# A graph layer's block pipeline: PSUM split by writer, sums a block later, layers two blocks later

## The chip, the core and the metric

The kernel runs on one core of a Trainium2 chip. The metric is the device time of one execution in microseconds, the median of three runs. A core has engines that run their own instruction streams and wait for each other by semaphores: TensorE (PE, matrix products, results into PSUM), VectorE (DVE), ScalarE (ACT), GpSimd (POOL) and SyncE (SP). Here POOL does almost nothing but issue gathers (indirect DMAs), SP and ACT issue DMAs, DVE does all the elementwise work.

## The reference

N = 50,000 nodes with D = 128 features, 1,650,000 edges sorted by destination, each of one of two types. Every edge sends its source's row through the weight matrix of its type; the messages are summed at the destination, a self term is added, then ReLU, a residual, and a layer norm.

```python
def _L0_gnn_ref(X, edge_index, edge_types, W_data, b_data, W_control, b_control, W_self, b_self):
    src = edge_index[0]
    dst = edge_index[1]
    Xs = X[src]
    m_data = Xs @ W_data.T + b_data
    m_ctrl = Xs @ W_control.T + b_control
    msg = jnp.where((edge_types == 0)[:, None], m_data, m_ctrl)
    agg = jax.ops.segment_sum(msg, dst, num_segments=X.shape[0])
    out = agg + (X @ W_self.T + b_self)
    return jax.nn.relu(out)

x = _layernorm(x + _L0_gnn_ref(x, edge_index, edge_type_2, ...), axis=-1)
```

## The kernel before

**Tiling.** The sorted edges are cut into 514 blocks (`NBLK`). A block is two steps (`Q`) of 12 chunks of 128 edges (`R`, `P`), so 24 chunks; each chunk's source rows are fetched by one gather of POOL (L555) into a buffer `y`. Besides these 3,072 edges a step takes 46 edges by "fill": edges of other places in the stream that are put into chunk rows which would have held a self loop (`F`, with `LATE` more for lateness), and 24 by single rows: DMAs of 512 bytes each, 12 issued by SP and 12 by ACT per step, so 24 each per block (L515 to L531), into `yx`. A block covers at most 112 destination nodes (`B`), a step at most 60 (`W`).

**Sums by product.** For each chunk, TensorE multiplies the gathered rows with a one-hot matrix `oh` (which of 60 destinations, which of two types) into a PSUM tile `acc`, one per step, accumulating over 12 chunks (`products`, L574), then the 24 single rows (L580), then the edge counts per destination and type for the biases (L583). A pass is six chunks (`PASS`), so a block has four passes, q = 0 to 3, and each pass has its own `y` from a ring of ten (`SLOTS`). `acc` comes from a ring of four, that is two blocks' worth. The gathers of a pass wait until the products that read the same buffer ten passes earlier are done; the first product of a pass waits for its six gathers.

**The rest of a block.** DVE adds each step's `acc` into the block's `sums` (`add`, L588; three `sums` tiles in turn). `begin_sums` (L599) starts a block's `sums` from the overlapping part of the block before and from `pl`, the correction for the self loops that the fill left out. `layer` (L613, L615) multiplies the finished sums by the two weight matrices into `po`, where `own_part` (L604, L605) has put the self term and the transposed row of `x`. `moments` (L620 to L628) takes ReLU, residual and mean and variance; `root` is a square root on ACT per two blocks, `store` (L647, L650) normalizes, `store_rows` (L655) writes 112 rows out from SP.

**Preparation.** Every ten blocks (`GB`) a group's edge lists are loaded and `columns` works out columns and ranks, for which TensorE makes `rank` (L298, L300) in a PSUM bank of its own from `h_loop` (L293, L294); DVE reads it at L323. Per block: `spread` (TensorE, L365) writes a list `vf` into the PSUM tile `small`; `fill` (DVE, L374 to L395) matches it, five blocks ahead (`RAHEAD`), giving the gathers' indices `idx` and `by`, the columns left out; `left_out_columns` (TensorE, L402) sums `by` into a column of `small`; `left_out_matrix` (DVE, L409, L410) reads that into `at` and makes `z`; `left_out_numbers` (TensorE, L418, L421) makes `pl` from `z`; `left_out_rows` (DVE, L427) multiplies `pl` by `xT`, a slice of transposed `x` that `positions` copies (L480) from a window `xw`. `onehot` and `counts` (DVE, L486, L494) make `oh` and `cnt` two blocks ahead (`AHEAD`); `onehot` reads a row of numbers, `num_ps`, that lies in the same PSUM tile `small` as `vf`, a copy `cb` (L374) and the sums of L402.

**Order.** Each engine runs its instructions in the order in which the code emits them; the framework puts a semaphore wait between an instruction and the last one on another engine that touched the same tile or, in PSUM, the same bank. One turn of the main loop, b, emits:

- before the passes: `spread` of the next fill, `add` of step 1 of block b-1, `begin_sums(b)`, `offsets`, `onehot(b+2)`, `counts(b+2)`
- pass 0, then `left_out_columns` and the `fill`, then 24 single rows on SP and ACT
- pass 1, then `layer(b-1)`, `left_out_numbers(b+1)`, `add` of step 0 of b, `moments(b-1)`, `left_out_matrix`, `positions(b+1)`, `left_out_rows(b+1)`, `store`
- pass 2 (with `columns` of the next group once in ten blocks), pass 3, `root`, `store_rows`

The adds read the `acc` of step 1 right after the last pass, at the start of the next turn, and that of step 0 after pass 1 of the same turn.

## Time and profile before

| | |
|---|---|
| median of three runs | 17,999.62 us (17,992.94 to 18,001.46) |
| the profiled execution's own time | 17,956.11 us |
| its span in the profile | 17,954.0 us |
| instructions in the trace | 165,064 |
| mean granted TensorE clock | 0.544 |
| gathers of POOL in the trace | 12,312 |
| moved by DMA | 913.88 MB, 51 GB/s on the mean |
| the chain of work that ended last | DVE 48%, unknown queue 27%, issue 15%, PE 10% |

The page's first part gives each engine's busy time and its share of the span. In a group's row, `out<-in` names the tiles, `x` counts instructions, then come the total busy time, the mean of one in ns, and the idle time of the engine just before these instructions with what ended it: "remote" is a message from another engine that the profile does not name, "issue" is time in which the engine waited for nothing that the profile shows. PEld is TensorE's loading of weights, which runs beside the products. A timeline row has the start, the duration, the engine and line, and in brackets the idle time ahead of it.

### The profile page before, as it was taken

What the parts mean: (1) busy time and instruction counts of PE and PEld (TensorE: products, weight loads), DVE (VectorE), ACT (ScalarE), POOL (GpSimd) and SP (SyncE); (2) the same over time, 40 slices, a digit from 0 to 9 for tenths busy, and PEclk for the clock granted to TensorE, in tenths of its full rate; (3) what the DMA queues carried; (4) which work ended last, traced back from release to release, by engine and by line L of the source; (5) the groups of instructions that cost most, each with busy time, mean ns of one, the idle gap of its engine ahead of it and who ended that gap; (6) DMA issues with size and microseconds to landing.
All of it is one profiled execution on the core that took longest, in us unless ns stands there. A gap on an engine that the chain in (4) does not pass through costs nothing.

```text
span 17954.0 us, 165064 instructions
## 1 busy us (share of the span) xinstructions
PE 8584.6 (48%) x37659; PEld 7319.4 (41%) x37660; DVE 12266.2 (68%) x14661; ACT 79.5 (0%) x264; POOL 11657.6 (65%) x12341
## 2 busy tenths in 40 slices
PE   4444444444444444444444444444444444544444
PEld 3444434444444444344444443444444443444434
DVE  7676666666666766666666676666666666766765
ACT  0000000000000000000000000000000000000000
POOL 6666666666666666666666666666666666666666
PEclk6555555555555555555555555555555555555555
DMA  2111212112122121111212211212221121121111
GB/s 54 51 50 51 52 50 51 51 51 51 50 52 51 50 52 50 51 51 51 51 50 52 51 50 51 51 51 51 51 51 50 51 52 50 51 52 50 51 50 50
DMA packets 529268, 913.88 MB, mean 51 GB/s; under 512 B 232762, under 2 KB 315875, under 8 KB 528274
## 3 DMA queue, kind: packets, MB, share of 16 engines
q0 software_dynamic: 394592, 808.89, 17.8%
q1 hardware_dynamic: 108668, 87.80, 1.7%
q10 hardware_dynamic: 25014, 6.54, 0.2%
q8 instruction: 306, 5.01, 0.1%
q14 instruction: 688, 5.64, 0.1%
HBM read 872.82 MB, written 29.47 MB: 50 GB/s over the span
## 4 chain that ended last, share of the span: by engine, by line
DVE 48%; another core or an unknown queue 27%; issue 15%; PE 10%; DVEq 0%; SPq 0%; DMA 0%; ACT 0%; ACTq 0%
DVE cnt L494 13%; DVE oh L486 7%; PE acc L574 7%; DVE m L376 4%; DVE v_new L383 4%; DVE new L379 4%; DVE old L392 4%; DVE sums L588 1%; DVE z L410 1%; DVE h L621 1%; DVE st L623 1%; PE acc L580 1%; PE po L615 1%; DVE xT L480 1%
## 5 line engine op out<-in xcount | busy, mean ns | idle before, releaser
L555 POOL DMA_INDIRECT y<-in_x,idx x12312 | 11638.2, 945 | 6265.2 <-issue 3408.4
L574 PEld LDWEIGHTS acc<-oh,y 128*128 128x128 f32 x24662 | 5348.8, 314 | 8255.9 <-issue 7977.9
L574 PE MATMUL acc<-oh,y 128*128 128x120 f32 x24662 | 5960.7, 412 | 3728.7 <-issue 3722.8
L588 DVE TENSOR_TENSOR sums<-acc,sums 128x180 f32 x1028 | 349.9, 340 | 4032.1 <-remote 3704.4
L494 DVE TENSOR_REDUCE cnt<-oh 128x240 bf16<-128x3120 f32 x514 | 3008.8, 5854 | 17.9
L402 PE MATMUL small<-ones_b,by 128*112 128x1 bf16 x512 | 83.4, 163 | 4177.0 <-issue 4045.0
L486 DVE TENSOR_TENSOR oh<-col,small 128x3120 f32<-128x3120 f32 x514 | 1740.6, 3386 | 43.8 <-remote 39.5
L395 DVE TENSOR_REDUCE by<-old 128x112 bf16<-128x1456 f32 x512 | 1426.7, 2787 | 17.5
L376 DVE TENSOR_TENSOR m<-rk,small 128x1456 f32<-128x1456 f32 x512 | 855.7, 1671 | 20.7 <-remote 2.4
L379 DVE TENSOR_TENSOR new<-m,small 128x1456 f32<-128x1456 f32 x512 | 855.2, 1670 | 17.5
L383 DVE TENSOR_REDUCE v_new<-new 128x26 f32<-128x1456 f32 x512 | 854.9, 1670 | 17.5
L392 DVE TENSOR_TENSOR old<-m,small 128x1456 f32<-128x1456 f32 x512 | 852.0, 1664 | 0.0
L580 PE MATMUL acc<-oh,yx 24*128 24x120 f32 x2048 | 758.1, 465 | 82.1 <-issue 82.1
L620 DVE COPY h<-po 112x128 f32<-112x128 f32 x514 | 145.3, 283 | 738.9 <-remote 622.6
L580 PEld LDWEIGHTS acc<-oh,yx 24*128 24x128 f32 x2048 | 487.3, 291 | 330.2 <-issue 319.1
L615 PE MATMUL po<-wmsgT,sums 128*112 128x128 f32 x2056 | 613.4, 453 | 3.7 <-issue 3.7
L365 PE MATMUL small<-v_f,row_of 10*128 10x112 bf16 x1536 | 223.2, 270 | 590.3 <-DVE at L409 197.6
L615 PEld LDWEIGHTS po<-wmsgT,sums 128*112 128x112 f32 x2056 | 448.8, 297 | 130.6 <-issue 129.9
L613 PE MATMUL po<-bias,sums 3*112 3x128 f32 x1028 | 391.4, 482 | 0.5 <-DVE sums L588 0.4
L365 PEld LDWEIGHTS <-row_of 10*128 10x128 bf16 x1536 | 122.8, 111 | 634.5 <-issue 592.7
L300 PEld LDWEIGHTS <-ones_b 128*128 128x128 bf16 x624 | 78.7, 149 | 671.3 <-issue 659.8
L298 PE MATMUL rank<-h_loop,below 128*128 128x260 bf16 x52 | 19.5, 375 | 672.7 <-DVE h_loop L294 357.8
(145 smaller groups left out, 5094.1 us busy)
## 6 DMA issues: line engine op xcount, KB each, us to landing
y<-in_x,idx POOLq DMA_INDIRECT x12312
yx<-in_x ACTq DMA_DIRECT2D x12288, 0.5 KB
yx<-in_x SPq DMA_DIRECT2D x12288, 0.5 KB
xw<-in_x_t SPq DMA_DIRECT2D x65, 448.0 KB
out<-o SPq DMA_DIRECT2D x514, 56.0 KB
sdt<-in_edges_t SPq DMA_DIRECT2D x52, 390.0 KB
one_g<-in_src_x SPq DMA_DIRECT2D x52, 1.9 KB
sdt_f<-in_edges_f SPq DMA_DIRECT2D x52, 13.1 KB
```

Source lines behind the costliest of these rows:

```text
L376: nc.vector.tensor_tensor(m, rk_g[g][:, i, :, None].to_broadcast([P, C1, FX]), rank_no_ps[:, None, :].to_broadcast([P, C1, FX]), op=ALU.is ...
L379: nc.vector.tensor_tensor(new.rearrange("p (q r) f -> p q r f", r=R1), m.rearrange("p (q r) f -> p q r f", r=R1), vf.rearrange("p (q f) -> ...
L383: nc.vector.tensor_reduce(v, new, AX.X, ALU.add)
L392: nc.vector.tensor_tensor(old, m, cb[:, :, None].to_broadcast([P, C1, FX]), op=ALU.mult)
L395: nc.vector.tensor_reduce(by, old.rearrange("p (q r) f -> p q f r", r=R1), AX.X, ALU.add)
L486: nc.vector.tensor_tensor(oh, col_g[g][:, i, :, None].to_broadcast([P, C1, 2 * W]), num_ps[:, None, :].to_broadcast([P, C1, 2 * W]), op=AL ...
L494: nc.vector.tensor_reduce(cnt, ohs[b].rearrange("p (q r) w -> p q w r", r=R1), AX.X, ALU.add)
L555: copy = nc.gpsimd.indirect_dma_start(out=y[:r, k % PASS, :].bitcast(U8), out_offset=None, in_=x_rows, in_offset=bass.IndirectOffsetOnAxis ...
L574: nc.tensor.matmul(acc[:, :2, :].rearrange("p t w -> p (t w)"), y[:r, k % PASS, :], ohs[b][:r, column(k), :], start=k == of_step[0], stop= ...
L580: nc.tensor.matmul(acc[:, :2, :].rearrange("p t w -> p (t w)"), ys[b][:, q, :], ohs[b][:S, q * R1 + R, :], start=False, stop=True)
L588: nc.vector.tensor_tensor(part, accs.pop((b, q)), part, op=ALU.add)
L615: nc.tensor.matmul(po, a[:, t, :B], c["wmsgT"][:, t * D:(t + 1) * D], start=False, stop=t == 1)
```

## The change

Four things are changed at once.

1. The PSUM tile `small` and `rank`'s bank become two tiles by the engine that writes them: `fixed` (DVE writes it: `num_ps`, `rank_no_ps` and the copies `cb`, now `olds`) and `made` (TensorE writes it: `vf`, `rank` and the sums of left-out columns). `vf` was two lists in turn and is now one.
2. `columns` is split: `loops` makes `h_loop` and `ranks` queues the rank products, one turn ahead of `columns`, which reads `rank`.
3. The order of a turn is new. Spread and fill stand back to back before pass 0. Both adds of a block, its `begin_sums`, `left_out_rows` and `positions` are emitted one turn later, after pass 2; the layer and the moments two blocks later than the products; `left_out_columns` after pass 2, behind `left_out_matrix` of the fill before.
4. `oh` and `cnt` have four buffers instead of three, `by` four instead of two, `xw` two instead of three. The first and last blocks are written out to match.

```diff
-    ohp = ctx.enter_context(tc.tile_pool(name="ohp", bufs=AHEAD + 1))
+    ohp = ctx.enter_context(tc.tile_pool(name="ohp", bufs=AHEAD + 2))
...
-    ps_r = ctx.enter_context(tc.tile_pool(name="ps_r", bufs=1, space=bass.MemoryType.PSUM))
...
-    small = keep_ps.tile([P, 2 * W + FX + 2 * FILL + 2], F32, name="small")
-    num_ps, rank_no_ps = small[:, :2 * W], small[:, 2 * W:2 * W + FX]
-    lists = [small[:, 2 * W + FX + i * FILL:][:, :FILL] for i in range(2)]
-    sums_at = [small[:Q * FX, 2 * W + FX + 2 * FILL + i:][:, :1] for i in range(2)]
+    fixed = keep_ps.tile([P, 2 * W + FX + 2 * C1], F32, name="fixed")
+    num_ps, rank_no_ps = fixed[:, :2 * W], fixed[:, 2 * W:2 * W + FX]
+    olds = [fixed[:, 2 * W + FX + i * C1:][:, :C1] for i in range(2)]
+    made_ps = keep_ps.tile([P, Q * FX + GS * (R + 1) + 2], F32, name="made")
+    vf_ps, rank = made_ps[:, :Q * FX], made_ps[:, Q * FX:Q * FX + GS * (R + 1)].rearrange("p (s r) -> p s r", r=R + 1)
+    sums_at = [made_ps[:Q * FX, Q * FX + GS * (R + 1) + i:][:, :1] for i in range(2)]
...
+    def loops(g):
...
+        nc.vector.tensor_tensor(h[:, :, :, :R], a["s"].rearrange(steps, r=R1)[:, :, :, :R],
+                                a["d"].rearrange(steps, r=R1)[:, :, :, :R], op=ALU.is_equal)
...
+    def ranks(g):
...
+        nc.tensor.matmul(rank, below, hs_, start=True, stop=False)
...
-        by = fil.tile([P, Q, FX], BF16, name="by")
+        by = fil.tile([P, Q, FX], BF16, name="by", bufs=4)
...
-        xw = stp.tile([P, WIDE], F32, name="xw")
+        xw = stp.tile([P, WIDE], F32, name="xw", bufs=2)
...
-        for f in fresh:
-            spread(f)
-        if b > 0:
-            add(b - 1, steps_of(b - 1)[-1])
-        begin_sums(b)
...
         offsets(b + AHEAD + 1)
         if b + AHEAD < NBLK:
             onehot(b + AHEAD)
             counts(b + AHEAD)
-        last = steps_of(b)[-1:]
+        if i == GB // 2 - 2 and g + 1 < GROUPS:
+            loops(g + 1)
+        for f in fresh:
+            spread(f)
+            fill(f)
         for q, (step, ks) in enumerate(passes_of(b)):
             if ks:
                 products(b, step, ks)
-            if q == 0:
+            if q == 1 and b > 0:
+                if b > 1:
+                    layer(b - 2)
+                left_out_numbers(b - 1)
+            if q == 2:
+                for f in late_pcs:
+                    left_out_matrix(f)
                 for f in due:
                     left_out_columns(f)
-                for f in fresh:
-                    fill(f)
-            if q == 1 and b > 0:
-                layer(b - 1)
-            if q == 1:
-                left_out_numbers(b + 1)
-            if ks and step not in last and ks[-1] == chunks_of(b, step)[-1]:
-                add(b, step)
-            if q == 1 and b > 0:
-                moments(b - 1)
-            if q == 1:
-                for f in due:
-                    left_out_matrix(f)
-            if q == 1 and b + 1 < NBLK:
-                positions(b + 1)
-                left_out_rows(b + 1)
-            if q == 2 and i == GB // 2 - 1 and g + 1 < GROUPS:
-                columns(g + 1)
-            if q == 1 and b > 1 and pair(b - 2):
-                store(pair(b - 2))
-                ready.extend(pair(b - 2))
+                late_pcs = due
+                if i == GB // 2 - 2 and g + 1 < GROUPS:
+                    ranks(g + 1)
+            if q == 2 and b > 0:
+                positions(b - 1)
+                left_out_rows(b - 1)
+                begin_sums(b - 1)
+                for step in steps_of(b - 1):
+                    add(b - 1, step)
+                if b > 1:
+                    moments(b - 2)
...
+                if b > 1 and pair(b - 2):
+                    root(pair(b - 2))
+                if i == GB // 2 - 1 and g + 1 < GROUPS:
+                    columns(g + 1)
             if q < LOADS and not plain(b + AHEAD):
                 single_rows(b + AHEAD, q)
-            if q == 3 and b > 0 and pair(b - 1):
-                root(pair(b - 1))
             if q == 3 and ready:
                 store_rows(ready.pop(0))
```

The rows below are the engines' orders in the middle of the program; in brackets stand the semaphores that a row waits for, named by the engine that raises them (`landed` is raised by gathers, `fetched` by single rows). Lines of the changed kernel are up to 8 higher: L402 of before is L409, L574 is L581, L588 is L595, L421 is L428, L486 is L493.

TensorE around passes 0 to 1 of one block, before:

```order
L365 MATMUL small<-v_f,row_of 128x112 [waits DVE_49]
...
L574 MATMUL acc<-oh,y 128x120 [waits landed8,PE_sequencer_49]
L574 MATMUL acc<-oh,y 128x120 x5
L402 LDWEIGHTS by
L402 MATMUL small<-ones_b,by 112x1 [waits DVE_49]
L574 MATMUL acc<-oh,y 128x120 [waits landed9,PE_sequencer_49]
L574 MATMUL acc<-oh,y 128x120 x5
```

TensorE from the layer after pass 1 to the first product of the next block, in the changed kernel:

```order
L622 MATMUL po<-wmsgT,sums_189 112x128 x2
...
L428 MATMUL pl<-z,to_row 128x128
...
L581 MATMUL acc<-oh,y 128x120 [waits landed0,PE_sequencer_49]
L581 MATMUL acc<-oh,y 128x120 x5
L409 LDWEIGHTS by
L409 MATMUL made<-ones_b,by 112x1 [waits DVE_49]
L581 MATMUL acc<-oh,y 128x120 [waits landed1,PE_sequencer_49]
...
L373 MATMUL made<-v_f,row_of 128x112
...
L581 MATMUL acc<-oh,y 128x120 [waits landed2,PE_sequencer_49,DVE_49]
```

The sum of left-out columns has moved from after pass 0 to after pass 2, with another wait for DVE ahead of it, and the first product of a block now waits for DVE as well.

VectorE over one block, before:

```order
L427 TENSOR_TENSOR pl<-pl,xT 128x2x112 [waits DVE_49,PE_49]
...
L588 TENSOR_TENSOR sums_191<-acc,sums_191 128x3x60 [waits PE_49]
...
L599 TENSOR_TENSOR sums_189<-pl,sums_191 128x3x112 [waits DVE_49]
...
L486 TENSOR_TENSOR oh<-col,small 128x3120 [waits PE_49]
...
L374 COPY small<-cb 128x26 [waits PE_49]
...
L395 TENSOR_REDUCE by<-old 128x112 [waits DVE_49]
...
L588 TENSOR_TENSOR sums_189<-acc,sums_189 128x3x60 [waits PE_49]
L620 COPY h<-po 112x128 [waits PE_49]
```

VectorE over one block, in the changed kernel:

```order
L402 TENSOR_REDUCE by<-old 128x112 [waits DVE_49]
L416 COPY at<-made 112x1
...
L434 TENSOR_TENSOR pl<-pl,xT 128x2x112 [waits DVE_49,PE_49]
...
L606 TENSOR_TENSOR sums_189<-pl,sums_188 128x3x112 [waits DVE_49]
...
L595 TENSOR_TENSOR sums_189<-acc,sums_189 128x3x60 [waits DVE_49]
...
L627 COPY h<-po 112x128
...
L493 TENSOR_TENSOR oh<-col,fixed 128x3120
...
L386 TENSOR_TENSOR new<-m,made 128x1456 [waits DVE_49,PE_49]
```

The adds, the one-hot matrix and the copy into `h` no longer wait for TensorE themselves; the product on `pl`, ahead of them, and `new` in the fill do.

More of the change, by code (lines that the diff above doesn't have):

```diff
@@ L174, in straight @@
     loads = {}
+    hs_g = {}
     col_g, rk_g, stay_g, cb_g, vp_g, late_g = {}, {}, {}, {}, {}, {}
@@ L288, in first_of_f @@
                    begin_p.rearrange("b (q g) -> b q g", q=Q)[:, :, g:g + 1].to_broadcast([GB, Q, FX]))
[L292 to L301 removed]
+        hs_ = hs_g.pop(g)
         col, rel, nz = columns_of(a["d"], a["t"], first_of, "")
@@ L688, in find_bad @@
         nc.vector.tensor_copy(c["bad"], total)
+    loops(0)
+    ranks(0)
     columns(0)
```

95 lines of the change are left out of this document (51 added, 44 removed).

## The prediction

> **What bounds the kernel now.** I read the page's first part, then the groups, the waits, the timeline of a block in the middle, and its windows. The profiled execution took 17,956 us (span 17,954.0); the median of the three timed runs is 43 us (0.24%) above it. The sums below are made against the execution, and the 43 us come on at the end.
>
> Rows of the page, then of the view by lines and of the waits (us in total, times, longest):
>
> ```profile
> PE 8584.6 (48%) x37659; PEld 7319.4 (41%) x37660; DVE 12266.2 (68%) x14661; ACT 79.5 (0%) x264; POOL 11657.6 (65%) x12341
> ...
> L555 POOL DMA_INDIRECT y<-in_x,idx x12312 | 11638.2, 945 | 6265.2 <-issue 3408.4 <-remote 2308.5 <-PE acc L574 182.3
> ```
> ```profile
> POOL y L555 <- issue: 3412.6, 11186, 0.7
> POOL y L555 <- remote: 2312.4, 778, 4.9
> ...
> POOL y L555 <- PE acc L574: 187.6, 109, 4.0
> POOL y L555 <- DVE old L392: 150.0, 53, 3.0
> ```
>
> POOL's gathers and the idle time ahead of them are 11,638 + 6,265 = 17,903 us, all but 51 us of the span, so POOL has no work but these. One gather costs 0.945 us busy and 3412.6/11,186 = 0.305 us of issue, 1.25 us together; 12,312 of them are 15,390 us, or 30.0 us for a block of 24. The other 17,903 - 15,390 = 2,513 us are pauses. The last three rows count 778 + 109 + 53 = 940 of them: 1.83 per block (514 blocks), each 2,513/940 = 2.67 us beyond the normal spacing. So POOL sets the pace, 34.8 us per block (17,903/514), of which 4.9 us are pauses. A gather pauses when the buffer it writes (10 passes back) has not been read by TensorE. So: what keeps TensorE?
>
> ```profile
> PE small L402 <- issue: 4045.0, 493, 25.8
> PE small L402 <- DVE oh L486: 132.1, 17, 21.7
> ...
> PE acc L574 <- issue: 3722.8, 2410, 3.3
> DVE sums L588 <- remote: 3704.4, 496, 18.1
> ```
> ```profile
> L365 PE MATMUL small<-v_f,row_of 10*128 10x112 bf16 x1536 | 223.2, 270 | 590.3 <-DVE at L409 197.6 <-issue 166.5 <-DVE h L620 88.9
> L298 PE MATMUL rank<-h_loop,below 128*128 128x260 bf16 x52 | 19.5, 375 | 672.7 <-DVE h_loop L294 357.8 <-DVE h_loop L293 210.2 <-issue 104.7
> ```
>
> Per block, TensorE is busy 8584.6/514 = 16.7 us. It waits 4,177/514 = 8.1 us ahead of L402, the one-column matmul after pass 0; 590.3/514 = 1.15 us at L365 and 672.7/514 = 1.3 us at L298. And 3722.8/514 = 7.2 us it stands between gathered matmuls for nothing that the profile shows. That is 34.5 us: the whole block is accounted for. The timeline shows both kinds of standing:
>
> ```profile
> 9010.52 2.92 PE L574 MATMUL acc<-oh,y 128*128 128x120 f32 x12
> 9015.65 0.16 PE L402 MATMUL small<-ones_b,by 128*112 128x1 bf16 x1 [2.21 <-issue]
> ...
> 9019.31 0.28 PE L583 MATMUL acc<-cnt,to_row 128*128 128x60 bf16 x2
> ...
> 9020.89 1.20 PE L615 MATMUL po<-wmsgT,sums 128*112 128x128 f32 x4
> ...
> 9022.10 0.42 PE L421 MATMUL pl<-z,to_row 112*128 112x128 bf16 x2
> ...
> 9026.46 0.36 PE L574 MATMUL acc<-oh,y 128*128 128x120 f32 x1 [1.29 <-issue]
> 9029.26 0.36 PE L574 MATMUL acc<-oh,y 128*128 128x120 f32 x1 [2.44 <-issue]
> ```
> ```profile
> 9011.32 0.34 DVE L588 TENSOR_TENSOR sums<-acc,sums 128x180 f32 x1
> 9011.69 0.51 DVE L599 TENSOR_TENSOR sums<-pl,sums 128x336 f32<-128x336 f32 x1
> ...
> 9012.21 3.38 DVE L486 TENSOR_TENSOR oh<-col,small 128x3120 f32<-128x3120 f32 x1
> 9015.63 5.86 DVE L494 TENSOR_REDUCE cnt<-oh 128x240 bf16<-128x3120 f32 x1
> ...
> 9037.73 0.34 DVE L588 TENSOR_TENSOR sums<-acc,sums 128x180 f32 x1 [5.99 <-remote]
> 9042.77 0.29 DVE L620 COPY h<-po 112x128 f32<-112x128 f32 x1 [4.69 <-remote]
> ```
>
> First, L402 starts at 9015.65, when `oh` ends (9012.21 + 3.38 = 9015.59), though it reads only `by`: both use the PSUM tile `small`. `oh` stands behind the adds L588 and L599, and L588 behind the last products of the block before. So the wait is one link of a ring: products, add, `oh`, L402, products.
>
> Second, a pass of 12 matmul records takes 2.92 us at 9010.52, but single records come 2.8 us apart from 9026. The windows show that this goes with POOL issuing (columns: us; PE, PEld, DVE, ACT, POOL busy with counts; clock, DMA share, GB/s):
>
> ```profile
> 9020.00:9025.00 5.00, 5.00 (x23) 4.32 (x21) 4.93 (x4) 0.00 (x0) 3.78 (x5) 0.50 0.21 53
> 9025.00:9030.00 5.00, 0.89 (x3) 0.57 (x2) 4.83 (x6) 0.00 (x0) 3.78 (x5) 0.50 0.20 53
> 9030.00:9035.00 5.00, 0.83 (x3) 0.86 (x3) 1.75 (x1) 0.00 (x0) 2.46 (x3) 0.50 0.14 40
> 9035.00:9040.00 5.00, 1.32 (x4) 1.15 (x4) 0.34 (x1) 0.00 (x0) 3.78 (x5) 0.50 0.22 53
> 9040.00:9045.00 5.00, 3.25 (x13) 2.21 (x13) 1.72 (x8) 0.29 (x1) 1.71 (x3) 0.50 0.12 33
> ```
>
> From 9025 to 9040 TensorE finishes 10 matmuls in 15 us, 0.67 per us against 12/2.92 = 4.1: a sixth of its speed, at an unchanged clock of 0.50, while DVE runs on. It recovers in the window where POOL pauses. I call this the crawl. Its messages crawl too: L583 ends at 9019.6 and the add that needs it starts at 9037.73, 18.1 us later; L615 ends at 9022.1, L620 starts at 9042.77, 20.7 us later.
>
> The Trainium skill speaks against such a crawl: "SBUF — State Buffer", Who interferes with whom, states that PE and ACT never wait on anyone there. These windows disagree; what the rule would make of the time is rival three.
>
> **A budget for TensorE.** A run of POOL between pauses is 30.0/1.83 = 16.4 us on the mean, and the crawl in it 7.2/1.83 = 3.9 us, so TensorE is fast for about the first 12.5 us of a run and for the 2.67 us of the pause. With n passes (7.5 us each) per run, TensorE gets 15.2 + (7.5n - 12.5)/6 us of fast time and needs 16.7/4 = 4.2 us per pass. What is left may go to waits: at n = 2 passes 7.2 us per run (14.4 per block), at n = 2.67 5.3 (8.0), at n = 3 4.3 (5.7), at n = 4 1.3 (1.3). Now n is 2.19 and the waits are 10.55 per block: the budget gives 6.65 per run, 12.2 per block, near enough to use it for differences.
>
> **The change, part by part.** No matmul, DVE operation or gather is removed: the records per block stay, and no time comes from doing less.
>
> *`oh` in another PSUM tile, the adds later.* L402 (now L409) no longer waits for `oh`, and `oh` no longer stands behind this block's products. Of the 10.55 us of waits, L402's 8.1 go. They lay on the path, since the ring fed the buffers that POOL waits for.
>
> *`by` late, sums read in the same tile.* In the new order L409 stands after pass 2 and DVE copies `at` out of the same PSUM tile, behind the whole fill, just ahead of it; so L409 waits for this block's `oh`, counts and fill. Behind L409 stand passes 3 and 0, the spread and the layer. And DVE's product on `pl` waits for L421 (now L428) of the same block. What DVE does from that product to the next `at` is read off here:
>
> ```profile
> 9021.42 0.17 DVE L374 COPY small<-cb 128x26 f32<-128x26 f32 x1
> ...
> 9028.97 2.78 DVE L395 TENSOR_REDUCE by<-old 128x112 bf16<-128x1456 f32 x1
> ...
> 9043.85 0.12 DVE L409 COPY at<-small 112x1 f32<-112x1 f32 x1
> ...
> 9044.96 0.40 DVE L427 TENSOR_TENSOR pl<-pl,xT 128x224 f32<-128x224 f32 x1
> ...
> 9046.15 3.39 DVE L486 TENSOR_TENSOR oh<-col,small 128x3120 f32<-128x3120 f32 x1
> ```
>
> From the product to `oh` 9046.15 - 9044.96 = 1.2 us, and the second add (0.34) and the moments (9043.85 - 9042.77 = 1.1) now stand there too; `oh` and counts 9021.42 - 9012.21 = 9.2; the fill 9028.97 + 2.78 - 9021.42 = 10.3: together 22.1 us. TensorE comes to L409 one block (say 33.5 us) and one pass (2.9) after the L421 of the block before, 36.4 us. If L421's message is late by d, L409 waits d + 22.1 - 36.4 = d - 14.3 us, nothing if that is below zero. The trace does not show d for L421. The lower end is d = 0, no wait; the upper end is the lag of 20.7 us above, a wait of 6.4. I take 5, near the upper end, because L421 stands next to the L615 that lagged so, and not the end itself, because both lags were seen in one crawl.
>
> *The ranks split out, one `vf` for two.* `h_loop` is made before the ranks' matmuls are queued and `rank` is read a block later, so L298's 1.3 us go. The spread waits for DVE's reads of the same tile as before, and for `rank` in one block of ten; its 1.15 us I leave.
>
> *More `oh` and `by` buffers, `xw` one fewer.* They cost nothing: `oh` at AHEAD + 2 only keeps a buffer for the later reader, and `xw` is loaded once in 8 blocks, three blocks ahead; without that cover it would be one DMA wait in 8 blocks. SP's and ACT's single rows stay behind pass 0. The new prologue and epilogue move a few block-ends, under 50 us in all, which I cost at nothing.
>
> *Sum.* Waits per block go from 10.55 to 5 + 1.15 = 6.15. The budget allows that at n = 2.93; scaled by what it misses today (10.55 where it says 12.2), at n = 2.78, which is 1.44 pauses per block. The upper end of d gives 7.55 us of waits, n = 2.56 and 1.56 pauses. I take the middle, 1.5: 0.33 pauses fewer, 0.33 x 2.67 x 514 = 453 us; 17,956 - 453 = 17,503, and with the 43 us about **17,550**. With no wait at L409 n would go to 4 (one pause, 0.83 x 2.67 x 514 = 1,139 saved: 16,860). An even three passes per run gives 1.33 pauses and 17,310; 1.75 pauses give 17,890. DVE bounds nothing: 12266.2/514 = 23.9 us of work per block.
>
> **Rivals.**
>
> *One, no change.* POOL needs its pauses for TensorE to recover, and whatever is freed turns into crawl; or L409 takes over all that L402 waited (9.4 us, from d = 23.7). For it: the crawl has no cause in the trace, and 940 pauses are regular. Against: the 8.1 us are true idle time. It gives 17,965 to 18,035.
>
> *Two, slower: the ring of `acc`.* There are four `acc`, two blocks' worth. Pass 0 of block b+1 now needs the add of block b-1, which DVE makes in block b, behind the product on `pl`, which waits for L421 of block b. TensorE needs one pass, 2.9 us, and then from 9015.65 to the end of L421 at 9022.52 6.9 us; DVE's product, begin and two adds are 0.40 + 0.51 + 2 x 0.34 = 1.6. The ring takes 11.4 + d, so it decides from d = 34.8 - 11.4 = 23.4 us on. At 20.7 it hides; but longer runs of POOL mean longer crawls, and the longest wait at L402 was 25.8 us. At 24.5, halfway, the block takes 35.9 us, 1.1 x 514 = 565 us more: 18,565; at 25.8 it is 19,230. Against it: before, the lags cost a ring only where DVE's `oh` closed it.
>
> *Three, all pauses go.* If the crawl does not follow POOL's runs, TensorE needs 16.7 + 7.2 + 6.15 = 30.05 us, no more than POOL's 30.0, and POOL is left: 15,390 + 51 + 43 = 15,480. By the skill's rule on PE and ACT it would come out here. Against it: the windows.
>
> *Four, SP.* Its 24 single rows and a store:
>
> ```profile
> 9013.35 29.91 SPq L529 DMA_DIRECT2D yx<-in_x  x24
> 9043.43 0.34 SPq L655 DMA_DIRECT2D out<-o  x1
> 9045.62 29.29 SPq L529 DMA_DIRECT2D yx<-in_x  x24
> ```
>
> take 9045.62 - 9013.35 = 32.3 us per block. With one pause or fewer this queue may bound: (34.8 - 32.3) x 514 = 1,285 saved, 16,715. With the one-pause case it fills 16,700 to 17,250.
>
> **How the numbers follow.** A difference under about 0.2% (36 us) can't be told from none here. Forecast, 17,250 to 17,890, likeliest 17,550: 46%. Four and one pause: 15%. Three: 3%. A gain of under 110 us: 2%. Faster is 66%. One, no change: 10%. Two, slower: 24%, of which I put a third below 18,250. The range runs from 16,800 to 18,250; it leaves out three, a part of four and two thirds of two, about 2 in 10. The forecast's own range is 17,250 to 17,890.
>
> **What would show it.** Right: PE's idle time ahead of L409 between 2,000 and 3,700 us (L402: 4,177), `sums` on DVE (now L595) near none, POOL's pauses about 770 (940), gathers still 945 ns. POOL's pauses at 500 with SP busy throughout would be rival four. DVE waiting at `pl` (L434) for over 10 us a block and passes waiting at DVE's adds would be rival two. The prediction fails if the crawl grows by more than L402 gives back, which the groups would show as "issue" ahead of L581 above 6,500 us.

## The result: no change worth having, 0.12% slower

The changed kernel takes 18,017.33 us (median of 20 runs, 18,008.55 to 18,023.25), the kernel before 17,995.74 us (20 runs, 17,989.94 to 18,001.70). The ratio is 1.0012, 95% interval 1.0005 to 1.0019. The forecast was 17,550.

All but one of the experiments below ran where the same kernel before takes 15,462 to 15,466 us, because POOL there issues its gathers without a pause, so each is read against the kernel before that ran beside it; nothing in the traces says what decides this.

First the first comparison. POOL after, from the view by lines and the waits (in the waits: us in total, times, longest):

```profile
L562 POOL DMA_INDIRECT y<-in_x,idx x12312 | 11677.1, 948 | 6276.5 <-issue 3439.1 <-remote 2145.6 <-PEq L569 314.4
```
```profile
PE acc L581 <- issue: 6234.2, 4530, 3.3
...
DVE pl L434 <- remote: 3618.1, 360, 31.4
POOL y L562 <- issue: 3443.0, 11268, 2.1
POOL y L562 <- remote: 2149.5, 742, 6.4
```

A gather's issue is 3443.0/11,268 = 0.3056 us, so of POOL's idle 6,276.5 us 12,312 x 0.3056 = 3,762 are issue and 2,514 are pauses. By the same sum the kernel before has 6,265.2 - 3,756 = 2,509. The pauses have moved by only 5 us in 2,500. The two profiled spans, 17,954.0 and 18,017.2 us, are 63 us apart (the medians 22): 39 are gathers (948 ns each, not 945), 11 their idle time, and 13 lie outside both.

Three groups of the kernel before, from its page (TensorE ahead of L402 and of the layer, DVE ahead of the adds), then TensorE and DVE after, from the view by lines:

```profile
L588 DVE TENSOR_TENSOR sums<-acc,sums 128x180 f32 x1028 | 349.9, 340 | 4032.1 <-remote 3704.4
...
L402 PE MATMUL small<-ones_b,by 128*112 128x1 bf16 x512 | 83.4, 163 | 4177.0 <-issue 4045.0
...
L615 PE MATMUL po<-wmsgT,sums 128*112 128x128 f32 x2056 | 613.4, 453 | 3.7 <-issue 3.7
```
```profile
L581 PE MATMUL acc<-oh,y 128*128 128x120 f32 x24662 | 6081.0, 399 | 6271.6 <-issue 6234.2
...
L434 DVE TENSOR_TENSOR pl<-pl,xT 128x224 f32<-128x224 f32 x512 | 204.7, 400 | 4231.0 <-remote 3618.1
...
L622 PE MATMUL po<-wmsgT,sums 128*112 128x128 f32 x2056 | 539.4, 383 | 365.4 <-issue 365.3
L409 PE MATMUL made<-ones_b,by 128*112 128x1 bf16 x512 | 91.2, 179 | 1295.1 <-issue 649.8
...
L373 PE MATMUL made<-v_f,row_of 10*128 10x112 bf16 x1536 | 228.8, 272 | 654.2 <-DVE runs L337 280.9
L620 PE MATMUL po<-bias,sums 3*112 3x128 f32 x1028 | 329.5, 397 | 166.9 <-issue 166.2
L595 DVE TENSOR_TENSOR sums<-acc,sums 128x180 f32 x1028 | 355.0, 345 | 40.9 <-PE acc L590 5.6
```

The change did what it says. TensorE waits 1,295 us ahead of L409, where it waited 4,177 ahead of L402, and DVE waits 41 us for the adds' operands, where it waited 4,032. (The page calls most of L402's wait "issue", but it was a wait for `oh`: 510 of the 512 times TensorE stood idle ahead of it, and each time L402 started 0.05 us after `oh` had ended.) Both came back elsewhere. "Issue" ahead of the gathered products rose from 3,723 to 6,234 us, and matmuls that had almost no such idle time before, the layer's L622 (3.7 before) and L620 (0.5), now have 365 and 167. DVE's wait stands at the product on `pl`, 4,231 us. All idle time of TensorE ahead of its matmuls is 9,361 us before and 9,545 after. The new idle time is no wait for another engine that the trace shows: of the 6,272 us ahead of the gathered products after, 5,466 stand ahead of products that have no semaphore to wait for (3,405 of 3,729 before).

The timeline of one stretch of the changed kernel, TensorE and then POOL (of POOL's rows only the first after a pause):

```profile
9006.81 0.69 PE L622 MATMUL po<-wmsgT,sums 128*112 128x128 f32 x4
9007.51 0.27 PE L425 MATMUL pl<-z,ones_b 112*128 112x256 bf16 x1
9008.95 0.22 PE L428 MATMUL pl<-z,to_row 112*128 112x128 bf16 x1 [1.17 <-issue]
9011.08 0.22 PE L428 MATMUL pl<-z,to_row 112*128 112x128 bf16 x1 [1.91 <-issue]
...
9015.33 0.36 PE L581 MATMUL acc<-oh,y 128*128 128x120 f32 x1 [1.76 <-issue]
9016.04 2.49 PE L581 MATMUL acc<-oh,y 128*128 128x120 f32 x10 [0.35 <-issue]
```
```profile
8998.63 0.95 POOL L562 DMA_INDIRECT y<-in_x,idx  x1 [2.86 <-remote]
...
9016.30 0.94 POOL L562 DMA_INDIRECT y<-in_x,idx  x1 [2.63 <-remote]
```

POOL resumes at 8998.63. TensorE runs fast up to 9007.8, and then, with no wait that the profile shows, one matmul in 2.1 us, until POOL pauses ahead of 9016.30. (Ahead of 9000.70 it had stood for 13.16 us behind `columns`, as in one block of ten; all stretches are counted below.) My reading: it had less to wait for, was done sooner with what it may do fast, and crawled for the rest.

I worked out two tables from the trace's rows, for both kernels. A pause is a gap of over 1.7 us from one gather's start to the next's, and its length runs from the end of the one to the start of the other. There are 924 of them before and 942 after. The first table puts those with whole passes between them in order by the passes that POOL issued since the last one:

| passes since the last pause | before: times, mean pause us | after: times, mean pause us |
|---|---|---|
| 1 | 152, 1.98 | 146, 2.18 |
| 2 | 432, 2.78 | 452, 2.76 |
| 3 | 311, 3.76 | 290, 3.75 |
| 4 | 23, 4.79 | 23, 4.75 |

The second has the mean count of instructions that TensorE (weight loads, without the matmuls beside them), SP and ACT (register loads too) started from one pause's end to the next's:

| passes in between | before | after |
|---|---|---|
| 2 | 101 | 103 |
| 3 | 119 | 117 |

The order of the work is new and these counts are not, within about 2%. That is weaker than it looks: both kernels run the same instructions and pause about as often, so the mean over all pauses had to agree; the table adds that it agrees for each length. What is new is the length of the fast stretch. Take the first idle time of over 0.2 us ahead of a gathered product that the profile calls issue: in the median it begins 13.9 us after POOL resumes in the kernel before (584 of 923 stretches have one), and 7.8 us in the changed one (716 of 941).

### The profile page after: what moved, and what is told of

The parts are those of the page before. It is cut to its first block, busy times and chain, and to the rows that moved or that the text cites. A ratio compares the mean times of both kernels' runs of the same rounds, so it can differ in the third digit from the quotient of the medians.

```text
span 18017.2 us, 166032 instructions
## 1 busy us (share of the span) xinstructions
PE 8463.9 (47%) x37659; PEld 7085.7 (39%) x37660; DVE 12239.6 (68%) x14661; ACT 79.6 (0%) x264; POOL 11696.6 (65%) x12341
## 4 chain that ended last, share of the span: by engine, by line
DVE 47%; issue 19%; another core or an unknown queue 19%; PE 13%; PEld 1%; DVEq 0%; DMA 0%; PEldq 0%; ACT 0%; ACTq 0%; SPq 0%
DVE cnt L501 11%; PE acc L581 9%; DVE oh L493 7%; DVE by L402 6%; DVE new L386 3%; DVE v_new L390 3%; DVE m L383 3%; DVE old L399 3%; DVE sums L595 1%; PE acc L587 1%; PE po L622 1%; DVE sums L606 1%; DVE z L417 1%; PEld acc L581 1%
## 5 line engine op out<-in xcount | busy, mean ns | idle before, releaser
L562 POOL DMA_INDIRECT y<-in_x,idx x12312 | 11677.1, 948 | 6276.5 <-issue 3439.1
L581 PE MATMUL acc<-oh,y 128*128 128x120 f32 x24662 | 6081.0, 399 | 6271.6 <-issue 6234.2
L581 PEld LDWEIGHTS acc<-oh,y 128*128 128x128 f32 x24662 | 5344.5, 303 | 7683.7 <-issue 7118.6
L434 DVE TENSOR_TENSOR pl<-pl,xT 128x224 f32<-128x224 f32 x512 | 204.7, 400 | 4231.0 <-remote 3618.1
L493 DVE TENSOR_TENSOR oh<-col,fixed 128x3120 f32<-128x3120 f32 x514 | 1739.1, 3383 | 0.0
L386 DVE TENSOR_TENSOR new<-m,made 128x1456 f32<-128x1456 f32 x512 | 855.7, 1671 | 960.8 <-remote 899.1
L402 DVE TENSOR_REDUCE by<-old 128x112 bf16<-128x1456 f32 x512 | 1429.2, 2791 | 17.6
L383 DVE TENSOR_TENSOR m<-rk,fixed 128x1456 f32<-128x1456 f32 x512 | 855.6, 1671 | 19.8 <-remote 2.3
L399 DVE TENSOR_TENSOR old<-m,fixed 128x1456 f32<-128x1456 f32 x512 | 851.1, 1662 | 0.0
L622 PE MATMUL po<-wmsgT,sums 128*112 128x128 f32 x2056 | 539.4, 383 | 365.4 <-issue 365.3
L409 PE MATMUL made<-ones_b,by 128*112 128x1 bf16 x512 | 91.2, 179 | 1295.1 <-issue 649.8
L622 PEld LDWEIGHTS po<-wmsgT,sums 128*112 128x112 f32 x2056 | 382.1, 244 | 502.6 <-issue 474.9
L373 PE MATMUL made<-v_f,row_of 10*128 10x112 bf16 x1536 | 228.8, 272 | 654.2 <-DVE runs L337 280.9
L620 PE MATMUL po<-bias,sums 3*112 3x128 f32 x1028 | 329.5, 397 | 166.9 <-issue 166.2
L595 DVE TENSOR_TENSOR sums<-acc,sums 128x180 f32 x1028 | 355.0, 345 | 40.9 <-PE acc L590 5.6
L590 PE MATMUL acc<-cnt,to_row 128*128 128x60 bf16 x2056 | 276.3, 219 | 80.1 <-issue 79.8
L612 PE MATMUL po<-wselfT,xT 128*112 128x128 f32 x1028 | 274.1, 350 | 79.6 <-issue 79.2
```

What stands on the lines that cost most here:

```text
L383: nc.vector.tensor_tensor(m, rk_g[g][:, i, :, None].to_broadcast([P, C1, FX]), rank_no_ps[:, None, :].to_broadcast([P, C1, FX]), op=ALU.is ...
L386: nc.vector.tensor_tensor(new.rearrange("p (q r) f -> p q r f", r=R1), m.rearrange("p (q r) f -> p q r f", r=R1), vf.rearrange("p (q f) -> ...
L399: nc.vector.tensor_tensor(old, m, cb[:, :, None].to_broadcast([P, C1, FX]), op=ALU.mult)
L402: nc.vector.tensor_reduce(by, old.rearrange("p (q r) f -> p q f r", r=R1), AX.X, ALU.add)
L493: nc.vector.tensor_tensor(oh, col_g[g][:, i, :, None].to_broadcast([P, C1, 2 * W]), num_ps[:, None, :].to_broadcast([P, C1, 2 * W]), op=AL ...
L562: copy = nc.gpsimd.indirect_dma_start(out=y[:r, k % PASS, :].bitcast(U8), out_offset=None, in_=x_rows, in_offset=bass.IndirectOffsetOnAxis ...
```

## The experiments

Three theories were put against each other. *Shared path*: instructions of TensorE, SP and ACT go through something that POOL's gathers starve; it passes so many per run and per pause, and the order of the work does not enter. *Gathers alone*: the pauses follow from the number of gathers. *Ring*: the freed wait went into a new one, at `pl`. Against the ring, the first comparison already shows that most of TensorE's idle time stands ahead of products without a semaphore to wait for.

### Single rows left out; half the matmuls; short gathers

`a_no_rows` and `b_no_rows`, the changed kernel and the one before without the rows' DMAs:

```diff
     def single_rows(b, part):
-        if part == 0:
-            ys[b] = stp.tile([S, Q, D], F32, name="yx", bufs=ROW_SLOTS)
...
+        ys[b] = yx_all
...
     def rows_fetched(b):
...
+        return
```

> The changed kernel without the DMAs of the single rows on SP and ACT (the rows' tile is filled with zeros once; TensorE's matmuls on it stay; the single rows' edges are left out of the sums). Three theories of why the new order changed nothing. Shared path: TensorE, SP and ACT share a path that POOL's gathers starve, and POOL's pauses are the time that this path needs for a fixed number of instructions; 98 of the 183 instructions per block on these three go, so most pauses go: 15,500 to 16,400 us. Gathers alone: a pause grows with the number of gathers before it whatever the others do (after 1, 2, 3, 4 passes it is 2.1, 2.8, 3.8, 4.8 us in the trace): 17,600 to 18,050. Ring: the wait went from L402 to DVE's product on pl, L434, and single rows play no part: 17,900 to 18,050.

> The kernel before, without the DMAs of the single rows in the same way (their edges are left out of the sums). Shared path: 15,500 to 16,800, and now, with the crawl mostly gone, the old order's wait at L402 may show as a difference to the changed kernel without the rows, in which case this one is slower by up to 800 us. Gathers alone: 17,600 to 18,050. Ring: as long as before, 17,900 to 18,050.

`a_half_mm`:

```diff
         for k in ks:
+            if k % PASS >= 3 and not plain(b):
+                continue
```

> The changed kernel with only 3 of the 6 matmuls of every pass (half of the gathered rows are fetched and left out of the sums). Shared path: 12 of 183 instructions per block (with the matmuls beside their weight loads 24 of 256) go from the three engines: 16,900 to 17,700. Gathers alone: 17,900 to 18,050. Ring: TensorE reaches L428 and the ends of its passes earlier by about 5 us of its own work per block and with half the crawl: 15,900 to 17,000.

`a_short`:

```diff
-            r = REST_ROWS[k] if b == NBLK - 1 else SIZES[k % R]
+            r = REST_ROWS[k] if b == NBLK - 1 else 64
```

> The changed kernel with gathers of 64 rows instead of 128 (as many gathers and matmuls, half of the edges are left out of the sums). If POOL's descriptors or their data load the path, the crawl and the pauses shrink: 15,500 to 17,000, and a gather on POOL may be shorter than 0.945 us as well. If it is the count of gathers or the instructions of TensorE, SP and ACT: 17,800 to 18,050. Ring: 17,800 to 18,050.

Measured, one run each: 15,456 us, 15,462, 15,472 and 14,937, and the kernel before beside them 15,462.5. These four therefore tell nothing of the three theories: there was no pause to remove. They do give POOL's price undisturbed, and `a_short` shows that a gather of 64 rows takes 905 ns and one of 128 rows 947, so that by these two points nearly all of a gather is a fixed cost.

### The change where POOL does not pause

`after_again` is the changed kernel itself.

> The changed kernel as it is, against the kernel before on the same chip. The four runs above had no pause in POOL at all, and the kernel before took 15,462 us beside them where it had taken 18,000. If pauses belong to the chip and not to the order: where POOL pauses, both kernels near 18,000 and within 0.3%; where it does not, both at 12,331 gathers x 1.25 = 15,410 plus about 50 us, and within 0.2%. If the new order matters where POOL does not pause: faster by more than 0.2%, which POOL's issue time leaves no room for.

Measured: 15,465.37 us against 15,465.63, ratio 0.9999 (0.9990 to 1.0009). POOL and TensorE in it, from the view by lines and the waits:

```profile
L562 POOL DMA_INDIRECT y<-in_x,idx x12312 | 11662.2, 947 | 3755.1 <-issue 3735.4 <-DVE fixed L381 8.8 <-DVE idx L394 6.1
```
```profile
PE acc L581 <- PEq L569: 6252.8, 1912, 6.4
...
DVE pl L434 <- PE pl L428: 2724.2, 448, 17.8
```

POOL's idle time is now all issue, 11,662 + 3,755 = 15,417 of 15,457 us. TensorE waits at L569, which is its wait for the gathers' data, and ahead of products without a semaphore to wait for it has no idle time of over 0.2 us. A kernel that is POOL's from end to end has no time to give to an order of the other engines.

`a_no_rows_2` repeated the run without single rows beside it: 15,457.6 us.

> The changed kernel without the DMAs of the single rows (left out of the sums), once more. Where the kernel before takes about 18,000 us beside it, shared path: 15,450 to 16,400; gathers alone: 17,600 to 18,050; ring: 17,900 to 18,050. Where the kernel before takes 15,460, no theory expects anything but 15,450 to 15,470.

### POOL out of the way

`a_half_g` and `b_half_g` issue 3 gathers per pass and use each twice:

```diff
+        ks = [k for k in ks if k % PASS < 3 or plain(b)]
         for k in ks:
...
-            nc.tensor.matmul(..., y[:r, k % PASS, :], ohs[b][:r, column(k), :],
+            nc.tensor.matmul(..., y[:r, k % PASS if plain(b) else k % 3, :], ohs[b][:r, column(k), :],
```

> The changed kernel with 3 gathers per pass instead of 6, each gathered chunk used by two matmuls (half of the edges are left out of the sums, the others are taken with wrong columns). POOL then needs 24/2 x 1.25 = 15.0 us per block and is no bound; TensorE, DVE, SP and ACT do as before. Shared path starved by gathers: the starving goes, the bound is DVE's 23.9 us of work per block or the ring over L409 and L428: 12,300 to 13,500. If gathers have nothing to do with the crawl: 15,500 to 18,000.

> The kernel before with 3 gathers per pass in the same way (half of the edges are left out, the others taken with wrong columns). With POOL out of the way this measures the old order's ring, products, add, one-hot, L402: TensorE's 16.7 us plus what the ring adds of DVE's add, begin and one-hot (about 7 us) is 24 us at least, DVE's 23.9 plus its wait for the add 30: 13,300 to 15,400, so slower than the changed kernel in the same state by 500 to 2,500 us. If the old wait at L402 was never more than a shift of the crawl: the same as the changed kernel within 1%.

Measured: 12,775 us for the changed kernel and 12,606 for the kernel before, one run each: the new order is 1.3% slower, where I had expected it to win by 500 us or more. `a_half_g`, its page and its waits:

```profile
PE 6678.5 (52%) x37659; PEld 5923.0 (46%) x37660; DVE 12243.3 (96%) x14661; ACT 79.5 (1%) x264; POOL 5857.9 (46%) x6197
```
```profile
PE made L409 <- DVE at L416: 5616.1, 508, 17.1
POOL y L563 <- PE acc L582: 5264.0, 1037, 13.9
```

`b_half_g`, the same:

```profile
PE 7784.8 (62%) x37659; PEld 6850.7 (54%) x37660; DVE 12135.3 (96%) x14661; ACT 79.5 (1%) x264; POOL 5847.1 (46%) x6197
```
```profile
PE small L365 <- DVE at L409: 2683.3, 457, 16.1
...
PE small L402 <- DVE oh L486: 1557.5, 510, 24.8
```

DVE is busy for 96% in both, so the old ring, which I had put at 24 to 30 us a block, costs next to nothing when messages are prompt: the block takes 12,606/514 = 24.5 us, of which DVE works 23.6. The new order pays 5,616 us of waits at L409, for the fill that it stands behind now. With DVE the bound this is nearly all beside DVE's work; of the 169 us between the two, 108 are DVE's own busy time (12,243.3 and 12,135.3), and what makes that longer stays open.

### More single rows

Where POOL is the bound, fewer gathers make a faster kernel, and each single row more per step makes a block hold more edges. `b_s72` has 72 single rows per step:

```diff
-TURNS = (12, 12)
+TURNS = (36, 36)
 S = sum(TURNS)
-LOADS = 1
+LOADS = 4
```

> The kernel before with 72 single rows per step instead of 24 (36 per step from SP and 36 from ACT, issued in four parts of a block's turn); the computation is whole. A block then takes 3,072 + 2 x (46 + 72) = 3,308 edges instead of 3,212, so 499 blocks instead of 514 and 499 x 24 = 11,976 gathers. Where POOL is the bound without pauses (the kernel before at 15,465): 11,976 x 1.25 + 50 = 15,030, 2.8% faster. Where POOL pauses (the kernel before at 18,000), shared path: about 192 more instructions of SP and ACT per block on a path that already holds the others up, 19,000 or more; gathers alone: 2.9% fewer gathers, 17,480.

Measured: 15,678 us against 15,462, ratio 1.0139 (1.0122 to 1.0156), slower, and no theory had it. SP's timeline says why:

```profile
9001.63 29.40 SPq L529 DMA_DIRECT2D yx<-in_x  x72
9031.20 0.34 SPq L655 DMA_DIRECT2D out<-o  x1
9033.23 27.89 SPq L529 DMA_DIRECT2D yx<-in_x  x72
9061.30 0.34 SPq L655 DMA_DIRECT2D out<-o  x1
9063.30 29.08 SPq L529 DMA_DIRECT2D yx<-in_x  x72
9093.34 0.34 SPq L655 DMA_DIRECT2D out<-o  x1
9095.29 4.85 SPq L529 DMA_DIRECT2D yx<-in_x  x15
```

A block's turn on SP takes (9095.29 - 9001.63)/3 = 31.2 us, more than POOL's 30.0, and 499 blocks of 31.2 are 15,570, all but 0.7% of the time. So 60 rows (`TURNS = (30, 30)`), `b_s60` and, in the new order, `a_s60`:

> The kernel before with 60 single rows per step (30 each from SP and ACT, in four parts); the computation is whole. With 72 rows SP's own turn was the bound: 31.3 us per block (9001.63, 9033.23, 9063.30, 9095.29 are its starts). 60 rows take 60/72 of the 29 us, with the gap of 2.4 us 26.6, under POOL's 30.0. A block takes 3,284 edges, so about 503 blocks, 12,060 gathers x 1.25 + 50 = 15,130: 2.2% faster than before where POOL does not pause. Where it pauses (18,000 beside it), shared path: slower, 19,000 or more; gathers alone: 2.2% faster.

> The changed kernel with 60 single rows per step in the same way. If POOL alone bounds: the same as b_s60 within 0.2%, 15,130. If the old wait at L402 (3,867 us with 72 rows) is on the path here: b_s60 slower than this one by 100 to 500 us. If the new waits (pl at L434, at ahead of L409) are on the path: this one slower.

Measured: 15,125 us, ratio 0.9783 (0.9767 to 0.9799), and 15,114, ratio 0.9775 (0.9758 to 0.9791), against 15,462. Both are as expected, and 60 rows are the one version with the whole computation that beats both kernels; it was measured only where POOL does not pause. L402 in `b_s60`, the view of one line:

```profile
its engine sat idle before it (us, times) until:
  DVE oh L486: 102.5, 56
  DVE by L395: 15.2, 1
  issue: 5.3, 2
```

That is 123 us of waiting ahead of L402 with the old order, where the same view of the profile of before has 4,242 (4,177 of them ahead of the matmul, the rest ahead of its weight load). The ring was there all the time; it was long where something ahead of the add came late. In the first comparison these were TensorE's messages. Where DVE stood waiting for the add, it started a median of 14.5 us after the product L583 had ended, and 0.04 us in `b_s60`. In `b_s72` they were the single rows: TensorE waits 4,519 us for them, and L402 waits 3,867 us for `oh` though the message to the add comes in 0.04 us.

### TensorE loaded to its limit

`a_pe3` and `b_pe3`, the products of the second step made three times:

```diff
+            for _ in range(2 if q == 1 and not plain(b) else 0):
+                nc.tensor.matmul(..., start=False, stop=False)
```

> The changed kernel with every gathered product of a block's second step made three times into the same sum (24 matmuls more per block, so the second step's sums are wrong). TensorE's own work goes from 16.7 to about 16.7 + 24 x 0.48 = 28.3 us per block, just under POOL's 30.0. If the new order does what the prediction said, no wait of TensorE lies in series with its work (no oh ahead of L409, and the waits at pl are DVE's): 15,470 to 15,600 where the kernel before takes 15,465. If L409's wait for at is in series: 16,000 or more. Where the kernel before takes 18,000 the longer work is paid in full: 19,500 or more.

> The kernel before with the same 24 matmuls more. If the old ring (last product, add, begin, one-hot 3.4 us, L402) is in series with TensorE's work: add, begin and one-hot take about 5 us after the last product, of which spread and pass 0 cover 3.4, so 28.3 + 2 to 4 us = 30.3 to 32.3 per block: 15,650 to 16,650, slower than a_pe3 by 100 us or more. If the wait at L402 was only slack that POOL left to TensorE: the same as a_pe3 within 0.3%.

Measured: 15,455.8 us (ratio 0.9996, 0.9985 to 1.0007) and 15,460.2 (0.9999, 0.9987 to 1.0010). The old ring, which by its theory was to show as 15,650 or more, costs nothing here either; L402 waits 217 us for `oh`. The test was weaker than meant: the granted clock rose from 0.51 to 0.69, and TensorE's own work came to 10,694/514 = 20.8 us a block (`b_pe3`), not 28.3. `a_no_rows_3` beside them took 15,458.5.

> The changed kernel without the DMAs of the single rows (left out of the sums), in case this chip pauses POOL as the first comparison's did. Where the kernel before takes about 18,000 us beside it, shared path: 15,450 to 16,400; gathers alone: 17,600 to 18,050. Where it takes 15,465: 15,450 to 15,470.

### The one experiment where POOL pauses

`a_s68` has 68 rows (`TURNS = (34, 34)`) in the changed kernel.

> The changed kernel with 68 single rows per step (34 each from SP and ACT, in four parts); the computation is whole. 501 blocks, 12,013 gathers x 1.25 + 50 = 15,070 if POOL still bounds; SP's turn is 68/60 x 23.3 us + 2.2 = 28.6 us, just under 30.0. If SP's turn, or rows that land too late, bounds already: 15,200 to 15,600. Where the kernel before takes about 18,000 beside it (a chip that pauses POOL), shared path: slower than 19,000; gathers alone: 17,550.

Measured: 24,153 us, and the kernel before beside it 17,867; ratio 1.3514 (1.3491 to 1.3537). Gathers alone, which asked for 17,550, has fallen; shared path had named the sign and a least size, 19,000. Two views, SP's timeline in three windows of 5 us and POOL's rows around them:

```profile
9003.61 3.50 SPq L536 DMA_DIRECT2D yx<-in_x  x3
...
9010.61 4.46 SPq L536 DMA_DIRECT2D yx<-in_x  x15
...
9033.95 3.57 SPq L536 DMA_DIRECT2D yx<-in_x  x3
```
```profile
9007.29 0.95 POOL L562 DMA_INDIRECT y<-in_x,idx  x1 [0.30 <-issue]
9023.92 0.94 POOL L562 DMA_INDIRECT y<-in_x,idx  x1 [15.69 <-PEq L569]
9025.17 0.94 POOL L562 DMA_INDIRECT y<-in_x,idx  x1 [0.30 <-issue]
...
9037.66 0.95 POOL L562 DMA_INDIRECT y<-in_x,idx  x1 [0.30 <-issue]
```

While POOL issues (9003 to 9008, and 9033 to 9038) SP gets 3 rows out in a window of 5 us; while POOL stands still, in between, 15. That is the crawl, on an engine that does nothing but issue DMAs and load registers. Over the whole trace the median step from one of SP's rows to the next is 1.09 us while gathers go out and 0.32 while POOL stands; in the kernel before, in the first comparison, 1.41 and 0.32; and in `b_s60` 0.32 beside the gathers. The wait that results, from the same run's waits:

```profile
PE acc L587 <- PEq L545: 17787.4, 499, 39.7
DVE pl L434 <- PE pl L428: 11324.8, 499, 34.7
POOL y L562 <- PEq L569: 4725.4, 300, 18.7
```

TensorE waits 17,787/499 = 35.6 us in every block for the single rows (L545 is its wait for them), and POOL waits for TensorE. Where POOL does not pause, SP issues such rows at 0.39 us each beside POOL's gathers, at the same rate of gathers. SP's rows in `b_s60` and in `a_half_mm`:

```profile
9021.38 23.11 SPq L529 DMA_DIRECT2D yx<-in_x  x60
```
```profile
9005.28 7.72 SPq L536 DMA_DIRECT2D yx<-in_x  x24
```

In the first comparison the kernel before took 29.9 us for the 24 that here take 7.7.

### What could not be settled

Three more runs were meant for a chip that pauses POOL.

> The changed kernel without the DMAs of the single rows (left out of the sums), for a chip that pauses POOL, as the last one did (68 rows per step: 24,153 us). Where the kernel before takes about 18,000 beside it, shared path: 15,450 to 16,400; gathers alone: 17,600 to 18,050; ring: 17,900 to 18,050. Where it takes 15,465: 15,450 to 15,470.

> The changed kernel with 3 gathers per pass, each gathered chunk used by two matmuls (half of the edges left out). If POOL's gathers are what starves TensorE, SP and ACT: near the 12,775 us of the chips that do not pause, under 13,500. If these three are slow by themselves on such a chip: 15,000 or more.

> The changed kernel with 4 single rows per step (2 each from SP and ACT); the computation is whole. A block takes 3,172 edges, so 521 blocks and 12,490 gathers, 12,490 x 1.25 + 50 = 15,660 us if POOL bounds. Where the kernel before takes about 18,000, shared path: 80 fewer instructions of SP and ACT per block, so most pauses go, 15,650 to 16,600, 8 to 13% faster; gathers alone: 1.3% more gathers, 18,200. Where the kernel before takes 15,465: 15,660, 1.3% slower.

None met one: the kernel before took 15,461.75 us beside them, and they took 15,462, 12,773 and 15,664 (ratio 1.0130, 1.0113 to 1.0147, as its 1.3% more gathers ask). So that the pauses go when the single rows go was not shown, and neither was a faster kernel for a chip that pauses.

The traces settle one rival: the DMA transfers themselves are no longer where POOL pauses. The packets of the gathers' queue took 17.8% of 16 engines' 17,954 us in the kernel before, 51,100 us in all, and 20.6% of 15,456.5 us, 50,900, in `after_again`; those of the two instruction queues took 0.1% each in both.

## Why the prediction was wrong, point by point

*What bounds the kernel.* POOL, with a floor of 30.0 us per block: right, and where nothing pauses it measures 15,465, the 15,480 that rival three gave. The 2,513 us of pauses were read rightly too, and so was L402's wait for `oh`. That TensorE recovers whenever POOL pauses was read too kindly: in the window from 9030 to 9035 POOL stood too (2.24 us ahead of 9033.01), and TensorE finished only 3 matmuls there.

*The accounting of TensorE.* The 34.5 us per block added up, but a sum that closes does not say which of its terms can be removed. All idle time of TensorE was 9,545 us afterwards where it had been 9,361, in other places.

*The step that failed* is the budget together with "L402's 8.1 go. They lay on the path". The budget took the crawl to begin a fixed 12.5 us after POOL resumes, so that a wait removed was fast time won. The traces show that the crawl began at 7.8 us, not 13.9, once TensorE had less to wait for, and that the three engines start as many instructions between two pauses as before. Removing the wait made TensorE reach the crawl sooner. No wait was mis-sized so as to explain the miss: those of L409, the ranks and the spread came to (1,295 + 242 + 654)/514 = 4.3 us a block, less than the 6.15 of the sum, and with 4.3 the budget would have given 1.28 pauses per block and about 17,240 us. Measured were 942/514 = 1.83 pauses, where the same count gives 1.80 for the kernel before. The wait itself was a consequence: with prompt messages it is 123 us, not 4,242. What made it long was the lateness of the message to the add, and that lateness now lies on the product on `pl`. What in the chip makes TensorE crawl, and why a wait removed comes back as crawl to within 2% of all idle time, stays open.

*The new waits.* L409 was put at 5 us a block; it waits 1,295/514 = 2.5. The lateness d of L428's message, which the sum could only bound by 0 and 20.7 us, can now be read: where DVE waits at `pl` (435 of 512 times), the product starts a median of 17.8 us after L428 has ended, and 0.04 us in `after_again`. L298's wait was to go; it fell from 673 us to 242 (57 and 185 at L289 and L291, the two lines of the ranks). The spread's stayed (654 us, 590 before), as said. `sums` waits 41 us, near none, as said. These steps were right, near it or on the safe side, and the result shows that they did not matter.

*Signs that the text named.* The prediction was to fail if the crawl grew by more than L402 gives back, and that is what it did: L409 waits 2,882 us less than L402 did, and the issue time ahead of L581, L620 and L622 grew by 3,039 us, from 3,727 to 6,766. The figure set for it, 6,500 us ahead of L581 alone, was not reached: there it is 6,234. L409 was to show 2,000 to 3,700 us and has 1,295. POOL's pauses were to fall to 770; counted as for the first table they are 942, and 924 before. DVE waits 8.2 us a block at `pl`, and passes wait 14.5 us in all for the adds: rival two stayed away.

*Rival one* fits what happened, both in the first of its two mechanisms ("whatever is freed turns into crawl"; L409 did not take over L402's wait) and in time (17,965 to 18,035), with a chance of 10%. Its argument, that the pauses were regular and the crawl had no cause in the trace, deserved more weight than the size of a wait.

*The Trainium skill's rule.* "SBUF — State Buffer", Who interferes with whom, in the Trainium skill says that PE and ACT never wait on anyone there. The runs at 15,465 us agree: in `after_again` TensorE has no idle time of over 0.2 us ahead of products without a semaphore. In the first comparison it has 5,466 us of it. No run shows which path it is, and it need not be a port of SBUF.

*What the theories come to.* That SP, ACT and TensorE are starved while POOL issues is shown for SP, by 3 rows against 15, and by the run with 68 rows; for TensorE by the windows of before and the crawl after; for ACT less clearly, by a median step from row to row of 0.56 us while gathers go out in the kernel before, against 0.32 in `b_s60`. That these engines share one budget of instructions is the reading that fits the two tables; it was not tested by taking instructions away. Nor was it tested, where POOL pauses, that fewer gathers end the slowness: what is shown is that it comes and goes with them.

## What to carry to other kernels

An idle time whose releaser is known, on a starved engine, is not yet time that can be won: first ask what made the releaser late, and whether all of the engine's idle time together has a cause outside the order of the work. Here the length of a pause followed the work since the last one and not the order of that work, and reordering did not move it. And a change is worth measuring in more than one condition: here 60 single rows per step instead of 24 win 2.2% where POOL does not pause, and 68 lose 35% where it does (60 were not run there).

## What the runs showed of the hardware that was not expected

The same kernel took 17,867 to 18,000 us or 15,462 to 15,466 us (medians), and runs listed under the same chip showed both, with no lower granted clock in the slower condition (0.54, against 0.51) and the same gather (945 ns in the kernel before in the one, 947 in `after_again` in the other): the difference that the traces show is that TensorE and SP slow down while POOL issues, and that TensorE's messages come late. The granted clock is not the same for all versions where POOL does not pause: 0.51 for the kernel as it is, 0.69 and 0.68 with 24 more matmuls per block, and 1.00 with gathers and products of 64 rows. The time of the POOL-bound kernel does not follow it: 15,456 to 15,465 us at 0.51 and at 0.69.
